# A Mamba-style layer with its chunk outputs laid out by channels instead of by tokens

## The chip, the cores and the metric

The kernel runs on one core of a Trainium2 chip. A core has TensorE (matrix multiply, PE in the profile; its weight loads are shown apart as PEld), VectorE (DVE), ScalarE (ACT), GpSimd (POOL) and SyncE (SP), which here issues the DMAs. The engines run at the same time and wait for each other through semaphores. The metric is the device time of one execution in microseconds (us); lower is better.

## The reference

The input is a batch of 8 images of 64 x 64 pixels with 192 channels. Two layers follow each other. Only the first is concerned; per image its 4096 pixels are a sequence of tokens:

```python
h = layernorm(xs, ln1_w, ln1_b)                  # xs = x + depthwise 3x3 conv
zxbcdt = h @ in_proj_w.T
z, xBC = zxbcdt[..., :384], zxbcdt[..., 384:896]
dt = softplus(zxbcdt[..., 896:] + dt_bias)       # 6 heads
xBC = silu(causal_conv1d(xBC))                   # xm 384, Bm 64, Cm 64
y = ssd(xm, dt, A, Bm, Cm)                       # state-space scan, 6 heads of 64
y = (y + xm * D_skip) * silu(z)
y = y * rsqrt(mean(y * y, -1) + 1e-5) * rms_w
x2 = xs + y @ out_proj_w.T
# then a second 3x3 conv, a layernorm and an MLP (192 -> 768 -> 192, gelu)
```

The scan is done in chunks. Inside a chunk a token's output is the sum over earlier tokens of (C·B) times a decay times dt·x; from the chunks before comes C times the carried state (64 x 64 per head), times the decay since the chunk began. After each chunk the state is decayed and the chunk's own contribution is added.

The second layer (a scan along four directions with another kernel structure) is the same in both kernels.

## The kernel before

**Tiling.** `layer0` goes over 64 tiles of 512 tokens (8 images x 8 tiles); each tile has 4 chunks of 128 tokens. All data are float32. `layer1` then takes the 8 images again.

**Layouts.** Activations lie mostly with channels on the partitions: 96 x 2 for the 192 channels, 128 x 3 for the 384. Some are turned, with the chunk's 128 tokens on the partitions: `zs` (silu of z), `xdt`, and the chunk output.

**One tile**, as a set of generators, with the tiles that the profile names:
- `gate` projects h to z and to the 6 dt columns, chunk by chunk with tokens on the output's partitions (`p_z`, 128 x 390, L531); `keep_gate` adds the dt bias (`dr`, L547) and takes the silu (`zs`, L550).
- `steps_in_time` makes dt (Abs, Exp, Ln), the cumulated decays (`p_c`, L588) and their exponentials `dec`; `rows_of` writes the cumulated sums as rows into a DRAM buffer `csd`, and `decays` loads them back spread over 128 partitions (`e`, L640).
- `powers` and `scores` turn `e` into the 128 x 128 matrix of each head (`e<-e,gm`, L682).
- `turn` transposes the conv output (`p_t`, L699) into `xdt` (L705) and `xw` (L710), and B into `bt`.
- `states` reads the carried state for the chunk (`p_i<-st,cm`, L740), multiplies by the decay (`t1`, L742), and forms the new state (`p_n`, L751; `st`, L761, L764).
- `mixer` forms the chunk output in one PSUM bank `py`: three matmuls with a diagonal matrix `dsk` for the skip term (L787), then six, one per head, with the head's matrix as the stationary operand and 64 columns of `xdt` moving (L790). VectorE adds `t1` (L803) and multiplies by `zs` (L806); ScalarE squares with a running sum (`sqj`, L814).
- `output` waits for the whole tile, computes the norm factor `rq`, scales the four chunk outputs on ScalarE (L843), transposes them back (`p_u`, L850), copies them (`yc`, L859), projects (`p_o`, L873), and adds the residual on VectorE into the padded image `xx` (L883).
- `mlp`, `norm2`, `conv2`, `norm1`, `conv1`, `mix`, `convolve`, `inputs` and `statistics` are the rest of the layer.

**Order.** Nothing is ordered by hand. `Flow` is a planner that runs at build time: every step has an engine, a weight in microseconds, and what it must wait for; buffers are counted slots that are taken and given back (`f.pool`). At each turn the step that can start first is emitted, a rank per generator breaks near-ties, and the order within each engine is then fixed in the program (`keep`). So each engine's queue is strictly in the planned order, and a wrong weight shows as a wait on the chip. `LAG`, `STAY`, `RANK` and the ranks are constants of this planner. PSUM has two pools here: "mm" with 5 banks for 512-column results, and "sm" with 3 banks shared by `p_t`, `p_b`, `p_g`, `p_i`, `p_n`, `p_y`, `p_u` and `p_c`. `xdt`, `xw` and `t1` have one buffer each.

Of the kernel before, what the change touches and what calls it, by code (L numbers as in the profile page):

```python
# [17 lines left out]
TT = 512  # L18
# [170 lines left out]
def layer0(tc, consts, x, x1s, mv1, w_in, w_out, w_fc1, w_fc2, rows):  # L189
# [12 lines left out]
    with ExitStack() as ctx:  # L202
# [39 lines left out]
        nc.vector.tensor_scalar_mul(an, an, -1.0)  # L242

        for i in range(3):
            nc.vector.tensor_scalar_mul(wo[:, i], wo[:, i], v128["rms"][:, i : i + 1])
        dsk = wp.tile([128, 3, 128], F32, name="dsk")
        for i in range(3):
            nc.vector.tensor_scalar_mul(dsk[:, i], ident, v128["dsk"][:, i : i + 1])
# [5 lines left out]

        f = Flow(tc)
        f.LAG, f.STAY, f.RANK = 0.684, -0.464, -0.01
        for tag, n in (("mm", 5), ("sm", 3), ("xin", 2), ("xs", 3), ("h", 3), ("cin", 2), ("cv", 2), ("zs", 2),
                       ("dt", 2), ("e", 5), ("yt", 4), ("yc", 1), ("xx", 3), ("x2", 1), ("m", 1), ("sq", 1), ("s2", 1), ("ld", 3), ("csr", 1), ("xdt", 1), ("xw", 1), ("t1", 1)):
            f.pool(tag, n)
# [255 lines left out]
        def gate():  # L515

            for T in range(len(tiles)):
                yield "wait", ("h1", T)
                yield "take", "zs"
# [3 lines left out]
                zs = got["zs", T] = tp.tile([128, NQ, DIN], F32, name="zs", bufs=2)  # L523
                for c in range(NQ):
# [4 lines left out]
                        1.35,  # L529
                        lambda: [  # L530
                            nc.tensor.matmul(  # L531
                                ps[:, : DIN + NH],
                                h[:, ct, c * Q : c * Q + Q],
                                wi[:, ct, 0 : DIN + NH],
                                start=ct == 0,
                                stop=ct == 1,
# [5 lines left out]
                    if c == NQ - 1:  # L542
                        h1_done(T, r)
                    f.fork(keep_gate(T, c, zs, dr, ps, r))

        def keep_gate(T, c, zs, dr, ps, r):
            q = yield step("DVE", 0.15, lambda: [nc.vector.tensor_add(dr[:, c], ps[:, DIN : DIN + NH], dtb)], r)  # L547
            if last := f.part(("dr", T), NQ, q):
                f.at["dr", T] = last
            r = yield step("ACT", 0.49, lambda: [nc.scalar.activation(zs[:, c], ps[:, :DIN], AF.Silu)], r, "silu")  # L550
            f.give("mm", max(q, r))
            if last := f.part(("zs", T), NQ, r):
                f.at["zs", T] = last

        def steps_in_time():

            for T in range(len(tiles)):
# [6 lines left out]
                    0.8,  # L564
                    lambda: [
                        nc.scalar.activation(dt, dr, AF.Abs),
                        nc.scalar.activation(dt, dt, AF.Exp, scale=-1.0),
# [9 lines left out]
                        nc.vector.scalar_tensor_tensor(dt, dr, 0.0, dt, ALU.max, ALU.add),  # L577
# [11 lines left out]
                        for i, m in enumerate((low, up, ones1))  # L589
# [4 lines left out]
                    "DVE", 0.16, lambda: [nc.vector.tensor_copy(cst.rearrange("p a b -> p (a b)"), pc[:, 24:48])], r  # L594
                )
                f.fork(rows_of(T, da))
                dec = got["dec", T] = sp.tile([128, 3, NQ, NH], F32, name="dec")
# [3 lines left out]
                    lambda: [nc.scalar.activation(dec.rearrange("p a b c -> p (a b c)"), pc[:, 0:72], AF.Exp)],  # L601
# [7 lines left out]
        def rows_of(T, da):  # L609
# [11 lines left out]
            csr = sp.tile([NH, TT], F32, name="csr", bufs=1)  # L621
            r = yield step("ACT", 0.6, lambda: [nc.scalar.copy(csr, ps[:NH])], r)
            f.give("mm", r)
            csd = got["csd", T] = dsp.tile([NH, TT], F32, name="csd")
# [7 lines left out]
        def decays():  # L632

            for T in range(len(tiles)):
                yield "wait", ("cs", T)
                for c in range(NQ):
                    yield "take", "e"
                    e = got["e", T, c] = ch.tile([128, NH, Q], F32, name="e", bufs=5)
                    src = got["csd", T][:, c * Q : c * Q + Q].partition_broadcast(128)
# [83 lines left out]

        def states():

            st = None
            for T, (b, t) in enumerate(tiles):
                yield "wait", ("w2", T)
                yield "wait", ("cv", T)
                dec, cm = got["dec", T], got["cm", T]  # L730
# [38 lines left out]
        def mixer():  # L769

            for T, (b, t) in enumerate(tiles):
# [3 lines left out]
                for c in range(NQ):  # L775
# [19 lines left out]
                    if c == 0:  # L795
                        yield "wait", ("zs", T)
# [1097 lines left out]
```

## Time and profile before

| what | value |
|---|---|
| three runs | 23742.58, 23752.58, 23754.5 us (median 23752.58) |
| the profiled execution | 23759.13 us, of which its span is 23757.4 us |
| busy over the span | PE 21089.6, DVE 21274.2, ACT 21040.0, POOL 16067.4 us |
| first layer: first 4868 us | PE 4496.60, DVE 3899.60, ACT 3178.97, POOL 704.51 us |
| second layer: the other 18889 us | PE 16593.03, DVE 17374.60, ACT 17861.01, POOL 15362.92 us |

The last group of matmuls of the first layer's MLP (L976) begins at 4857.54 us and lasts 10.46 us, and the first instruction of the second layer on GpSimd (L1057) stands at 4868.13 us; that is where the table divides. A float32 matmul appears as two records in the profile, each with its own weight load; a transpose appears as one. "PEclk" is the share of TensorE's clock that the throttle granted.

Durations of neighbouring instructions overlap in the timeline, since the next one starts before the last has drained. Where work follows without a wait, the distance from start to start is what an instruction costs its engine.

### The profile page before, as it was taken

The page shows a single profiled execution, that of the slowest core. Times are in us where ns is not written, and L with a number is a line of the kernel's source. Part 1 is how long each engine was busy: PE and PEld are TensorE (multiplying, and loading weights), DVE is VectorE, ACT ScalarE, POOL GpSimd, SP SyncE. Part 2 cuts the span into 40 slices and gives each one's busy share as a digit, 9 for nine tenths or more (in the row PEclk, how much of TensorE's full clock was granted, in tenths as well). Part 3 has the DMA queues.
Part 4 walks back from the last instruction along what each step waited for, and adds up shares of the span by engine and source line. Part 5 has one row for each costly group of instructions (what it writes and reads, how often), then busy time and mean ns, then how long its engine had stood idle before and what let it go on. Part 6 is the DMA issues. An engine that isn't in the chain of part 4 may idle for free.

```text
span 23757.4 us, 313126 instructions
## 1 busy us (share of the span) xinstructions
PE 21089.6 (89%) x100804; PEld 10279.5 (43%) x100804; DVE 21274.2 (90%) x22093; ACT 21040.0 (89%) x37507; POOL 16067.4 (68%) x12871
## 2 busy tenths in 40 slices
PE   7999999978888888888888888888888888888888
PEld 4444444434444444444444444444444444444444
DVE  7888888779998999899989998999899989998998
ACT  5666766669998999899989998999899989998998
POOL 1111111149995999599959985998699769976997
PEclk8999999989999999999999999999999999999999
DMA  2111111133233323333233233323332233233332
GB/s 50 45 44 44 46 44 43 39 99 81 81 79 107 81 82 78 107 81 82 76 112 81 82 77 109 81 81 79 110 82 81 78 107 82 81 85 100 82 83 67
DMA packets 1368290, 1859.75 MB, mean 78 GB/s; under 512 B 268576, under 2 KB 697024, under 8 KB 1357440
## 3 DMA queue, kind: packets, MB, share of 16 engines
q1 hardware_dynamic: 1366656, 1839.73, 28.7%
q8 instruction: 810, 13.27, 0.2%
q14 instruction: 824, 6.75, 0.1%
HBM read 1225.98 MB, written 210.50 MB: 60 GB/s over the span
## 4 chain that ended last, share of the span: by engine, by line
POOL 43%; PE 24%; ACT 15%; DVE 7%; issue 6%; DMA 4%; SPq 1%; POOLq 0%; ACTq 0%; DVEq 0%
POOL hc L1648 40%; ACT pw L1592 6%; ACT ea L1607 6%; POOL cy L1646 3%; PE p_f L956 3%; DMA xc<-xo 2%; DVE xs L1202 2%; PE p_f L976 2%; PE p_x L448 2%; PE y L1663 2%; PE p_o L873 2%; PE p_y L790 1%; PE g L1618 1%; PE p_d L1481 1%; PE p_z L531 1%
## 5 line engine op out<-in xcount | busy, mean ns | idle before, releaser
L1648 POOL TENSOR_TENSOR hc<-hs,cb 128x1024 f32<-128x1024 f32 x6144 | 14592.9, 2375 | 12.0 <-POOL cy L1646 9.9
L1634 DVE TENSOR_TENSOR_SCAN hs<-ea,cy,g 128x512 f32<-128x512 f32 x10752 | 13024.0, 1262 | 608.6 <-PE g L1618 411.1
L1592 ACT ACTIVATE pw<-duT,bt 128x384 f32<-128x384 f32 x16384 | 8874.1, 601 | 20.2 <-DVE duT L1539 20.2
L1607 ACT ACTIVATE ea<-dr,an 128x512 f32<-128x512 f32 x12288 | 8120.5, 709 | 189.2 <-DVE hs L1634 170.8
L1663 PE MATMUL y<-hc,sel 128*64 128x512 f32 x24576 | 6624.0, 617 | 1841.3 <-POOL hc L1648 1819.2
L1618 PEld LDWEIGHTS g<-ident,pw 128*128 128x128 f32 x49152 | 5288.7, 141 | 4336.8 <-issue 2671.4
L1618 PE MATMUL g<-ident,pw 128*128 128x128 f32 x49152 | 6788.4, 279 | 60.1 <-ACT pw L1592 28.6
L1646 POOL COPY cy<-hs 128x2 f32<-128x2 f32 x6144 | 1164.2, 189 | 3373.5 <-DMA out_x<-xl 1733.8
L1663 PEld LDWEIGHTS y<-hc,sel 128*64 128x64 f32 x24576 | 1225.9, 134 | 3254.1 <-POOL hc L1648 3031.3
L1634 DVE TENSOR_TENSOR_SCAN hs<-ea,g 128x512 f32<-128x512 f32 x1536 | 1763.7, 1202 | 159.0 <-PE g L1618 115.6
L365 POOL TENSOR_TENSOR s<-xs 96x512 f32<-96x512 f32 x64 | 121.1, 1892 | 2033.7 <-DVE xs L343 1522.9
L1202 DVE SCALAR_TENSOR_TENSOR xs<-pad,p,xs 128x4096 f32<-128x4096 f32 x192 | 860.9, 4484 | 43.4 <-ACT xs L1192 36.2
L1510 PE MATMUL p_dt<-xdbl,wd 13*128 13x512 f32 x1536 | 857.2, 639 | 41.0 <-DVE de L1523 39.1
L365 POOL TENSOR_TENSOR s<-sq 96x512 f32<-96x512 f32 x128 | 211.6, 1653 | 964.1 <-ACT sq L378 899.8
L1481 PE MATMUL p_d<-xc,wx 128*44 128x512 f32 x1536 | 791.6, 598 | 22.6 <-DMA xc<-xo 22.0
L343 DVE SCALAR_TENSOR_TENSOR x<-xx,p,x 96x512 f32<-96x512 f32 x1024 | 785.2, 815 | 19.4 <-ACT x L332 19.4
L956 PE MATMUL p_f<-h,wf 96*128 96x512 f32 x1536 | 761.9, 632 | 24.4 <-ACT zs L550 14.0
L343 DVE SCALAR_TENSOR_TENSOR xs<-xin,p,xs 96x512 f32<-96x512 f32 x1024 | 749.3, 767 | 4.6 <-ACT xs L332 4.6
L976 PE MATMUL p_f<-m,wf 128*96 128x512 f32 x1536 | 692.9, 601 | 0.0
L1532 PEld LDWEIGHTS p_du<-ident,de 128*128 128x128 f32 x3072 | 323.5, 141 | 610.2 <-DVE de L1523 405.8
L448 PE MATMUL p_x<-h,wi 96*128 96x512 f32 x1024 | 544.5, 664 | 12.3 <-ACT h L405 11.1
L365 POOL TENSOR_TENSOR s<-x 96x512 f32<-96x512 f32 x64 | 96.2, 1502 | 626.3 <-DVE x L343 477.2
(202 smaller groups left out, 19557.2 us busy)
## 6 DMA issues: line engine op xcount, KB each, us to landing
cb<-cd SPq DMA_DIRECT2D x4096, 128.0 KB
dr<-de SPq DMA_DIRECT2D x3072, 128.0 KB
xc<-xo SPq DMA_DIRECT2D x256, 768.0 KB
e<-csd SPq DMA_DIRECT2D x256, 384.0 KB
xl<-x SPq DMA_DIRECT2D x256, 384.0 KB
ut<-xo SPq DMA_DIRECT2D x128, 768.0 KB
ut<-xo SPq DMA_DIRECT2D x256, 384.0 KB
xo<-xs SPq DMA_DIRECT2D x48, 1024.0 KB
```

Source lines behind the costliest of these rows:

```text
L343: nc.vector.scalar_tensor_tensor(im(out[:, ct]), tap(ct, j), w[:, ct, j : j + 1], im(out[:, ct]), ALU.mult, ALU.add)
L956: nc.tensor.matmul(ps, wf1[:, ct, mt * 128 : mt * 128 + 128], h[:, ct], start=ct == 0, stop=ct == 1)
L976: nc.tensor.matmul(ps[:CP], wf2[:, kt, ct * CP : ct * CP + CP], m[:, kt], start=kt == 0, stop=kt == 5)
L1202: nc.vector.scalar_tensor_tensor(xs, tap(j), kw[:, d, j : j + 1], xs, ALU.mult, ALU.add)
L1481: nc.tensor.matmul(st["p_d"][:44], wx[:, d, k], st["xc"][:, d], start=d == 0, stop=d == DT - 1)
L1592: nc.scalar.activation(st["pw", p, j][:, :, i], st["duT"][:, j].rearrange("p (g c) -> p g c", c=64), AF.Copy, scale=st["bt"][:, j, n : n + 1],
L1607: nc.scalar.activation(ea[:, f], state[s]["dr", d][:, f], AF.Exp, scale=an[:, k, p, at : at + 1])
L1618: nc.tensor.transpose(g[:, f, j * 128 : j * 128 + 128], state[s]["pw", p, j][:, 2 * d + f].rearrange("p a b -> p (a b)"), ident,)
L1634: nc.vector.tensor_tensor_scan(rev(h[:, f]), rev(ea[:, f]), rev(g[:, f]), 0.0 if first(s) else state[s - 1]["cy"][:, p, d, f : f + 1], ALU ...
L1646: o(nc.gpsimd.tensor_copy(st["cy"][:, p, d], h[:, :, last]))
L1648: o(nc.gpsimd.tensor_mul(hc, h, bc(st["cb", p], 1, [128, 2, TT])))
L1663: o(nc.tensor.matmul(y[half[f]], sel, hc[:, f], start=p == 0 and k > 0, stop=p == NP1 - 1))
```

## The change

Only `layer0` changes, and in it six things.

1. **Chunk outputs by channels.** In `mixer`, `xdt` (64 columns of a head) becomes the stationary operand and the head's 128 x 128 matrix moves, so that the result has channels on partitions: 64 rows per head, even heads in rows 0 to 63 and odd heads in rows 64 to 127 of the same 128 columns. The transposes and copies in `output` go.
2. **The carried state in the same bank.** Six more matmuls with the state as stationary operand (64 x 64) add the state's part directly; `p_i` and `t1` go. What moves is C times the decay since the chunk began, one 64 x 128 matrix per head: the new generator `carried` loads the exponentials (`csd` has a second row set for them) over 64 partitions and multiplies them with C on GpSimd, in one buffer `ce`. The state has three buffers, as it is read later.
3. **Skip term on VectorE.** The diagonal matmuls go; three VectorE instructions per chunk form skip times conv output plus bank.
4. **z by channels**, in three groups of 512 tokens; the dt columns get their own matmuls (`p_dr`) with h as the stationary operand.
5. **The norm factor behind the projection.** The squares are summed over channels by a matmul with a matrix of 1/384 (`p_q`), in the new generator `squares`; the factor `rms` multiplies the projected result, and GpSimd adds the residual.
6. dt uses Exp and Ln without Abs; `dec` loses one of its three parts; the planner's constants and ranks are new.

```diff
         f = Flow(tc)
-        f.LAG, f.STAY, f.RANK = 0.684, -0.464, -0.01
+        f.LAG, f.STAY, f.RANK = 0.804, -0.31, -0.01
...
+                        nc.tensor.matmul(
+                            pd[:, c * NH : c * NH + NH],
+                            h[:, ct, c * Q : c * Q + Q],
+                            wi[:, ct, DIN : DIN + NH],
+                            start=ct == 0,
+                            stop=ct == 1,
+                        )
+                        for c in range(NQ)
+                        for ct in range(CT)
...
+                for i in range(3):
...
-                                ps[:, : DIN + NH],
-                                h[:, ct, c * Q : c * Q + Q],
-                                wi[:, ct, 0 : DIN + NH],
-                                start=ct == 0,
-                                stop=ct == 1,
+                                ps, wi[:, ct, i * 128 : i * 128 + 128], h[:, ct], start=ct == 0, stop=ct == 1
...
-                        nc.scalar.activation(dt, dr, AF.Abs),
-                        nc.scalar.activation(dt, dt, AF.Exp, scale=-1.0),
+                        nc.scalar.activation(dt, dr, AF.Exp),
                         nc.scalar.activation(dt, dt, AF.Ln, bias=1.0),
...
-                        nc.vector.scalar_tensor_tensor(dt, dr, 0.0, dt, ALU.max, ALU.add),
+                        nc.vector.scalar_tensor_tensor(dt, dt, BIG, dr, ALU.min, ALU.max),
...
-            r = yield step("ACT", 0.6, lambda: [nc.scalar.copy(csr, ps[:NH])], r)
+            r = yield step(
+                "ACT",
+                1.2,
+                lambda: [nc.scalar.copy(csr[:, 0], ps[:NH]), nc.scalar.activation(csr[:, 1], ps[:NH], AF.Exp)],
+                r,
+                "explog",
+            )
...
+        def carried():
+
+            for T, (b, t) in enumerate(tiles):
+                yield "wait", ("cs", T)
+                yield "wait", ("cv", T)
+                cm = got["cm", T]
+                for c in range(NQ):
+                    if t == 0 and c == 0:
+                        continue
+                    yield "take", "ce"
+                    ce = got["ce", T, c] = ch.tile([NS, NH, Q], F32, name="ce", bufs=CE)
+                    src = got["csd", T][:, 1, c * Q : c * Q + Q].partition_broadcast(NS)
+                    r = yield step("SP", 0.1, lambda: [nc.sync.dma_start(out=ce, in_=src)], f.at["cs", T])
+                    f.at["ce", T, c] = yield step(
+                        "POOL",
+                        2.0,
+                        lambda: [nc.gpsimd.tensor_mul(ce, ce, bc(cm[:, c * Q : c * Q + Q], 1, [NS, NH, Q]))],
+                        r + 3,
+                    )
...
-                        q = yield step("PE", 0.7, lambda: [nc.tensor.matmul(pi, cm[:, tk], st, start=True, stop=True)])
-                        q = yield step(
-                            "DVE", 0.55, lambda: [nc.vector.tensor_mul(hv(t1), hv(pi), bc(dec[:, 1, c], 2, heads))]
-                        )
...
-                        for i in range(3):
-                            cs = slice(i * 128, i * 128 + 128)
-                            f.keep(nc.tensor.matmul(py[:, cs], cv[:, i, tk], dsk[:, i], start=i == 0, stop=False))
-                        for hd in range(NH):
-                            cs = slice(hd * HD, hd * HD + HD)
-                            f.keep(nc.tensor.matmul(py[:, cs], e[:, hd], xdt[:, cs], start=False, stop=hd == NH - 1))
-
-                    q = yield step("PE", 2.2, out)
+                        for w, v in ((xdt, e), (st, ce)):
+                            for hd in range(NH) if w is not None else ():
+                                rows = slice(hd % 2 * 64, hd % 2 * 64 + 64)
+                                cs = slice(hd // 2 * 128, hd // 2 * 128 + 128)
+                                f.keep(
+                                    nc.tensor.matmul(
+                                        py[rows, cs],
+                                        w[:, hd * HD : hd * HD + HD],
+                                        v[:, hd],
+                                        start=w is xdt and hd < 2,
+                                        stop=hd >= NH - 2 and (w is st or st is None),
+                                    )
+                                )
+
+                    q = yield step("PE", 1.3 if st is None else 2.4, out)
...
+                            nc.vector.scalar_tensor_tensor(
+                                yc[:, i, tk], cv[:, i, tk], v128["dsk"][:, i : i + 1], yv[:, i], ALU.mult, ALU.add
+                            )
+                            for i in range(3)
...
+                    q = yield step("DVE", 0.6, lambda: [nc.vector.tensor_mul(yc[:, :, tk], yc[:, :, tk], zs[:, :, tk])])
...
+        def squares():
...
+                    r = yield step("ACT", 0.55, lambda: [nc.scalar.activation(sq, yc[:, :, tk], AF.Square)])
...
+                            nc.tensor.matmul(pq[:CP, tk], onesq, sq[:, i], start=i == 0, stop=i == 2) for i in range(3)
...
+                        nc.scalar.activation(rs, pq[:CP], AF.Ln, bias=eps[:CP]),
+                        nc.scalar.activation(rs, rs, AF.Exp, scale=-0.5),
...
-                    q = yield step("ACT", 0.62, lambda: [nc.scalar.activation(yt, yt, AF.Copy, scale=rs[:, c : c + 1])], r)
...
-                            nc.tensor.transpose(pt[:, i * 128 : i * 128 + 128], yt[:, i * 128 : i * 128 + 128], ident)
...
-                        lambda: [nc.scalar.copy(yc[:, :, c * Q : c * Q + Q], pt.rearrange("p (i q) -> p i q", i=3))],
...
-                        lambda: [nc.vector.tensor_add(xx[:, ct, 1 : RT + 1, 1 : WI + 1], im(ps[:CP]), im(xs[:, ct]))],
+                    r = yield step("DVE", 0.7, lambda: [nc.vector.tensor_mul(inner, im(ps[:CP]), im(rs))], p)
...
+                r = yield step(
+                    "POOL", 2.7, lambda: [nc.gpsimd.tensor_add(both, both, xs.rearrange("p t (h w) -> p t h w", w=WI))]
+                )
```

## The prediction

> **What bounds the kernel now.** I read the busy time by windows first, to see how much of the span the change can touch; then TensorE's timeline over one tile, for prices and gaps; then VectorE and GpSimd beside each other; last the order of the instructions in the two built programs.
>
> ```profile
> core 0: us, PE busy (x) PEld busy (x) DVE busy (x) ACT busy (x) POOL busy (x), PEclk, DMA share, GB/s
> 1000.00:4400.00 3400.00, 3212.36 (x11037) 1593.11 (x11037) 2808.96 (x4643) 2298.83 (x4436) 495.59 (x379) 0.93 0.18 45
> 2500.00:2515.00 15.00, 15.00 (x54) 7.21 (x52) 14.96 (x26) 8.75 (x22) 3.42 (x1) 1.00 0.69 170
> 2515.00:2534.00 19.00, 14.76 (x66) 10.39 (x66) 12.10 (x23) 12.71 (x30) 1.19 (x1) 0.70 0.01 1
> 2534.00:2575.00 41.00, 41.00 (x125) 18.52 (x124) 34.06 (x53) 29.74 (x48) 5.11 (x5) 0.97 0.04 10
> ```
>
> The first row is the steady part of the first layer, 46 tiles in 3400 us: 73.9 us a tile, TensorE busy 69.8 (94%), VectorE 61.1, ScalarE 50.0, GpSimd 10.8. TensorE bounds the layer. The other rows are one tile in three stretches: TensorE is full at full clock in two, and in the middle one it idles for 4.2 of 19 us at 0.70 of the clock. The layer takes 4868 us of 23757; the second layer's instructions don't change, so I price it at nothing.
>
> ```profile
> 2499.70 0.94 PE L787 MATMUL p_y<-dsk,cv 128*128 128x128 f32 x6
> 2500.47 1.45 PE L790 MATMUL p_y<-xdt,e 128*128 128x64 f32 x12
> 2501.85 0.86 PE L751 MATMUL p_n<-xw,bt 128*64 128x384 f32 x2
> 2502.64 0.55 PE L699 MATMUL p_t<-ident,cv 128*128 128x128 f32 x3
> 2503.02 1.02 PE L366 MATMUL ln_m<-s,ones 96*96 96x512 f32 x2
> ...
> 2505.69 0.91 PE L740 MATMUL p_i<-st,cm 64*128 64x384 f32 x2
> 2506.44 0.22 PE L715 MATMUL p_b<-ident,bm 64*128 64x64 f32 x1
> ...
> 2556.20 3.65 PE L448 MATMUL p_x<-h,wi 96*128 96x512 f32 x8
> 2559.69 5.40 PE L531 MATMUL p_z<-wi,h 96*128 96x390 f32 x16
> 2564.93 10.46 PE L976 MATMUL p_f<-m,wf 128*96 128x512 f32 x24
> ```
>
> From start to start, at full clock: the diagonal matmuls 0.77 us a chunk (0.128 a record), the heads 1.38 (0.115 a record, though only 64 columns move), `p_i` 0.75, a transpose 0.38/3 = 0.127, `p_z` 5.24 a tile, a 512-column record 3.49/8 = 0.436.
>
> ```profile
> 2519.83 0.27 PE L715 MATMUL p_b<-ident,bm 64*128 64x64 f32 x1 [0.78 <-DVE xw L710]
> 2522.49 0.69 PE L699 MATMUL p_t<-ident,cv 128*128 128x128 f32 x3 [1.10 <-DVE yt L803]
> 2524.87 1.54 PE L751 MATMUL p_n<-xw,bt 128*64 128x384 f32 x2 [1.06 <-DVE t L742]
> 2528.75 2.66 PE L790 MATMUL p_y<-xdt,e 128*128 128x64 f32 x12
> ```
>
> These rows lie in the middle stretch: `p_t` waits for the bank that `yt` frees, `p_n` for `t1`, and the heads' twelve records take 2.45 us (to 2531.20) instead of 1.38, since the clock has fallen after the gaps. Of such loss a tile has on average 4.1 us of idling and, at 0.93 of the clock, some 0.07 x 69.8 = 4.9 us of slow running.
>
> **What the skill says.** The Trainium skill, "TensorE: Matmul & The Clock Gate", "Part 3: Packing small matmuls", says that the output's start partition picks the column tile and that matmuls in different ones run concurrently. The second layer's `y` shows it: two matmuls of 64 rows each (four records of 512) take 6007.88 - 6006.98 = 0.90 us, as two records of `p_d` alone do (0.96):
>
> ```profile
> 6006.98 1.08 PE L1663 MATMUL y<-hc,sel 128*64 128x512 f32 x4
> 6007.88 1.02 PE L1481 MATMUL p_d<-xc,wx 128*44 128x512 f32 x2
> 6008.84 1.09 PE L1618 MATMUL g<-ident,pw 128*128 128x128 f32 x8
> ```
>
> Its "LDWEIGHTS" section says that a load's time goes with its columns, not its rows; the heads' records above (0.115 us for 64 moving columns behind 128-wide loads, against 0.128 for 128) agree. "SBUF — State Buffer", "Who interferes with whom", says that a VectorE instruction with two SBUF inputs and a GpSimd instruction that reads SBUF exclude each other for their whole length. The trace agrees: a conv step of 0.73 us takes 2.87 when it starts beside a GpSimd add.
>
> ```profile
> 2547.39 2.87 DVE L343 SCALAR_TENSOR_TENSOR xs<-xin,p,xs 96x512 f32<-96x512 f32 x1
> ```
>
> (GpSimd's `xr` add runs from 2547.37 for 2.34 us.) "TensorEngine Tiling (Array Packing)", "Key Properties", says that changing the tiling mode drains the array; `p_n` (64 wide) between 128-wide work takes 0.79 us for 768 columns, 0.65 by the 512-column price, so I put the drain under 0.14 and leave it out.
>
> **The change part by part, per tile.**
>
> TensorE removed: diagonals 4 x 0.77 = 3.1; heads 4 x 1.38 = 5.5; `p_i` 4 x 0.75 = 3.0; transposes `p_u` 12 x 0.127 = 1.5; `p_z` 5.2. Sum 18.3. Added: z by channels 12 records x 0.436 = 5.2; `p_dr` 16 records, each behind a 128-wide load, x 0.115 = 1.8; `p_q` 24 x 0.128 = 3.1; chunk outputs 24 records of 128 columns a chunk. The trace has no 128-column records side by side. If two run together as in `y`: 12 x 0.128 = 1.54 us a chunk, 6.2 a tile; if not, 3.07 and 12.3. I take the first: the column tiles alternate as in `y`, and the loads are half as wide. Added 16.3, or 22.4. Net -2.0 at full clock; divided by 0.93, **-2.2** (else +4.1/0.93 = +4.4).
>
> The loss in the middle stretch, 9.0 us: `p_u`, the ScalarE scaling and copy (twice four of 0.62 and 0.47), `t1` and the wait for the whole tile's norm go, and two users leave the three "sm" banks. Against that, `p_q` holds one of five "mm" banks from the first chunk to the factor. The bound is 0 to -9.0. The chain xdt, heads, bank, next xdt with its one buffer stays, so I take about a third, **-3.3**.
>
> VectorE: `t1` and the add (8 x 0.46, start to start) = -3.7; twelve skip steps of 128 columns at 0.2 (`gm`, the nearest row, starts 0.19 before its successor) = +2.4; three dt adds less, -0.3; the multiplication by `rms` replaces the add at equal size. Net -1.6. But GpSimd gets four `ce` multiplications (64 x 768; between 1.26 us at 512 and 2.34 at 1024 columns: 1.8) and the residual (2.3), 9.5 us with SBUF inputs. Today's 7.4 us of such work cost VectorE, by means over clean durations (16 steps of 0.82 against 0.73, 16 of 0.77, 4 each of `st`, `yt` and `e` 0.1 above theirs, two of `h` 0.08 above), 3.4 us a tile, 0.46 per us. So +4.4, and VectorE ends at 61.1 - 1.6 + 4.4 = 63.9. That is still below TensorE, so most hides; bound 0 to 4.4, I take **+1.0**.
>
> The `ce` loop: the next load may start only when the heads' matmuls have read `ce`; SP waits there with `xin`, `xl` and later loads queued behind it. The cost is the load, 1.8 us on GpSimd (plus a lock) and 1.5 for the matmuls. The nearest load, the first of four `e` twice as large, is issued at 2501.99 and waited for until 2508.26: at most 6.3. So a turn lasts up to 9.6 us. In the changed order the TensorE work between consecutive chunk outputs is, by these prices, about 5.5, 14, 10 and 32 us: only the first gap can be too short, by 0 to 4.1. I take **+0.6**; a load alone and half as large is quicker.
>
> ScalarE loses about 3 us of 50; table loads stay (431 and 427 in the two programs). It was never the bound: nothing beyond the relief above. Fill and drain of the pipeline: nothing.
>
> Sum: -2.2 - 3.3 + 1.0 + 0.6 = -3.9 us a tile, x 64 = -250 us. Against the profiled execution, 23759 - 250 = 23509; the median lies 6.5 lower: **23503**.
>
> **The rivals.**
> - *Heads not side by side* (slower). TensorE then gets +4.4 instead of -2.2: -3.9 + 6.6 = +2.7 a tile, +173: 23926. It decides from 1.54 + 3.9 x 0.93/4 = 2.45 us a chunk on. For it: each head has its own weights to load, where `y` loads the same ones; the planner's own weight for the step, 2.4, fits no overlap. Against: `y`.
> - *Given back on the port*: VectorE's 4.4 and the `ce` stall of 4.1 come in half (4.2 in place of 1.6), and the relief is 2.0: -2.2 - 2.0 + 4.2 = 0: 23753, no change. For it: the conv steps blocked above; against: VectorE has 12.8 us free a tile.
> - *The stretch closes*: 7 of the 9.0 us return, and the charges are 1.2: -8.0 a tile, -512: 23241. For it: the other two stretches run full at full clock; against: `xdt` keeps one buffer.
>
> **How the numbers follow.** Forecast 0.54 (own range 23370 to 23650), heads 0.22, port 0.12, stretch closes 0.12. This measurement can tell about 0.2%, 48 us. Faster: 0.54 + 0.12 + a third of the port case = 0.70; same 0.06; slower 0.22 + the port's other edge = 0.24. The range reaches down to 23260, by the closing stretch, and up to 23880, within the bad cases, leaving some 0.06 below and 0.13 above.
>
> **What would show it.** Right: six pairs of a chunk in some 1.5 us; TensorE busy near 67 us a tile of 70; the clock above 0.93; conv steps (L343) longer on average. Wrong: 24 records spread over 2.5 us or more; TensorE waiting on GpSimd's `ce` in front of the chunk output; tile time unchanged with more idling of TensorE behind VectorE.

## The result and the profile after

The changed kernel takes 24302.43 us (median of four runs, 24289.1 to 24322.3) beside 23753.33 (23742.58 to 23754.5): a ratio of 1.0231, 95% interval 1.0219 to 1.0243. It is 549 us slower where 250 us less were forecast, and the time lies above the range. The view of busy time by windows, divided where the second layer begins, and its steady part:

```profile
core 0: us, PE busy (x) PEld busy (x) DVE busy (x) ACT busy (x) POOL busy (x), PEclk, DMA share, GB/s
0.00:5402.00 5402.00, 4593.28 (x17752) 2242.08 (x17752) 4149.35 (x6537) 2992.88 (x5298) 1429.17 (x862) 0.87 0.21 49
5402.00:24298.90 18896.90, 16602.04 (x85532) 8045.86 (x85532) 17376.19 (x15634) 17871.04 (x31374) 15364.99 (x12323) 0.99 0.31 87
...
1000.00:4400.00 3400.00, 2936.58 (x11365) 1433.15 (x11364) 2695.84 (x4190) 1908.94 (x3395) 918.16 (x539) 0.87 0.21 49
...
2505.00:2518.00 13.00, 13.00 (x52) 5.84 (x50) 3.64 (x6) 6.10 (x10) 2.65 (x3) 1.00 0.11 30
2518.00:2536.00 18.00, 10.46 (x55) 7.00 (x56) 18.00 (x29) 4.45 (x8) 7.27 (x4) 0.57 0.09 23
2536.00:2550.00 14.00, 14.00 (x46) 6.88 (x47) 7.72 (x10) 7.42 (x13) 2.04 (x1) 0.69 0.00 0
```

The first layer has grown from 4868 to 5402 us, the second is the same within 8. In the steady part 41 tiles pass instead of 46: 82.9 us a tile instead of 73.9. TensorE's work has not grown: it is busy for 71.6 us a tile instead of 69.8, but at 0.87 of the clock instead of 0.93; times the clock, as an estimate, that is 62.3 us at full clock instead of 64.9. What has grown is its idling, (3400 - 2936.58)/41 = 11.3 us a tile instead of 4.1, and its slow running, 71.6 - 62.3 = 9.3 instead of 4.9. GpSimd has doubled, 22.4 instead of 10.8. The last three rows show part of one tile: TensorE is full at full clock, then idles for 7.5 of 18 us with a mean clock of 0.57, and is full again with the clock at 0.69.

The timeline from the end of the first of these stretches on (start, duration, line, tiles; in brackets idle time before and what ended it):

```profile
2516.32 0.88 PE L833 MATMUL p_y<-e,xdt 128*64 128x128 f32 x12
2517.12 0.87 PE L833 MATMUL p_y<-ce,st 64*64 64x128 f32 x12
2517.93 1.10 PE L366 MATMUL ln_m<-s,ones 96*96 96x512 f32 x2
...
2519.16 2.25 PE L528 MATMUL p_dr<-wi,h 96*128 96x6 f32 x16
...
2522.49 3.58 POOL L765 TENSOR_TENSOR ce<-ce,cm 64x768 f32<-64x768 f32 x1 [9.52 <-DMA ce<-csd]
...
2526.12 1.54 PE L833 MATMUL p_y<-ce,st 64*64 64x128 f32 x12 [0.94 <-POOL ce L765]
2527.60 1.59 PE L888 MATMUL p_q<-sqc,onesq 128*96 128x128 f32 x6
...
2532.12 7.13 DVE L343 SCALAR_TENSOR_TENSOR xs<-xin,p,xs 96x512 f32<-96x512 f32 x3
2532.31 2.21 POOL L765 TENSOR_TENSOR ce<-ce,cm 64x768 f32<-64x768 f32 x1 [6.24 <-DMA ce<-csd]
2534.48 1.26 POOL L365 TENSOR_TENSOR s<-sq 96x512 f32<-96x512 f32 x1
2535.70 2.34 POOL L975 TENSOR_TENSOR xr<-xr,x 96x1024 f32<-96x1024 f32 x1
2535.79 2.02 PE L366 MATMUL ln_v<-s,ones 96*96 96x512 f32 x2 [6.60 <-POOL s L365]
```

The first three rows answer the question of the heads: both sets of twelve records take 2517.93 - 2516.32 = 1.61 us. Two heads do run side by side. The other rows show what costs. TensorE waits 0.94 us for `ce`, and then 6.60 us for `s`, the sum of squares of a layernorm. `s` has nothing to do with `ce`; it stands behind the next multiplication in GpSimd's queue, and that one waits for its load. The clock is another matter. Windows cut at its steps give 1.00 up to 2520.65 us, 0.50 up to 2544.55 and 1.00 after that. So it fell during the sixteen `p_dr` records, before either wait: TensorE had no gap from 2495.81 to 2525.19 us. It stayed low for 8.8 us after TensorE was full again. The chain of waits gives the same stretch in order (start, duration):

```profile
2516.39 1.63 PE p_y L833 x24
...
2518.07 4.28 DMA ce<-csd
...
2522.49 3.59 POOL ce L765
...
2526.12 1.57 PE p_y L833 x12
...
2527.74 4.41 DMA ce<-csd
...
2534.48 1.27 POOL s L365
...
2535.79 2.02 PE ln_v L366 x2
```

One turn through the single buffer is the load, the multiplication and the matmuls, 2527.74 - 2518.07 = 9.7 us. The waits of the steady part, summed (us in total, times, longest), in the changed kernel:

```profile
POOL ce L765 <- DMA ce<-csd: 1289.5, 138, 21.5
...
PE ln_v L366 <- POOL s L365: 101.5, 25, 7.9
PE p_q L888 <- ACT sqc L883: 65.1, 23, 5.3
PE ln_m L366 <- POOL s L365: 62.0, 16, 8.6
PE p_y L833 <- DVE st L800: 61.2, 18, 5.7
PE p_y L833 <- POOL ce L765: 34.2, 18, 5.2
...
SPq L761 <- PE p_y L833: 1697.8, 135, 45.9
```

and in the kernel before:

```profile
PE ln_v L366 <- POOL s L365: 7.3, 2, 6.8
PE ln_m L366 <- POOL s L365: 6.7, 6, 3.5
```

TensorE waits 34.2 us for `ce` (0.8 a tile) but 101.5 + 62.0 = 163.5 for `s` (4.0 a tile; 14.0 us in the kernel before), and 65.1 for `sqc`, the squares of a chunk output (1.6 a tile). SP stands half of the time before a `ce` load.

### The profile page after: what moved, and what is told of

It is laid out like the page before. It is cut to its first block, busy times and chain, and to the rows that moved or that the text cites. A ratio compares the mean times of both kernels' runs of the same rounds, so it can differ in the third digit from the quotient of the medians.

```text
span 24298.9 us, 318148 instructions
## 1 busy us (share of the span) xinstructions
PE 21195.3 (87%) x103284; PEld 10287.9 (42%) x103284; DVE 21525.5 (89%) x22170; ACT 20863.9 (86%) x36671; POOL 16794.2 (69%) x13184
## 4 chain that ended last, share of the span: by engine, by line
POOL 42%; PE 20%; ACT 17%; DVE 7%; issue 6%; DMA 6%; SPq 2%; POOLq 0%; ACTq 0%; DVEq 0%
POOL hc L1701 37%; ACT pw L1645 7%; ACT ea L1660 7%; POOL cy L1699 3%; DMA xc<-xo 2%; DVE xs L1255 2%; PE p_f L1027 2%; PE y L1716 2%; DMA ce<-csd 2%; PE p_f L1007 2%; PE p_x L448 2%; PE g L1671 1%; PE p_z L558 1%; PE p_y L833 1%; PE p_o L921 1%
## 5 line engine op out<-in xcount | busy, mean ns | idle before, releaser
L1660 ACT ACTIVATE ea<-dr,an 128x512 f32<-128x512 f32 x12288 | 8185.5, 719 | 181.8 <-DVE hs L1687 165.9
L765 POOL TENSOR_TENSOR ce<-ce,cm 64x768 f32<-64x768 f32 x248 | 649.1, 2617 | 2386.0 <-DMA ce<-csd 2047.5
L343 DVE SCALAR_TENSOR_TENSOR xs<-xin,p,xs 96x512 f32<-96x512 f32 x1024 | 856.1, 868 | 85.6 <-ACT xs L332 85.6
L343 DVE SCALAR_TENSOR_TENSOR x<-xx,p,x 96x512 f32<-96x512 f32 x1024 | 845.1, 863 | 38.1 <-ACT x L332 38.1
L1007 PE MATMUL p_f<-h,wf 96*128 96x512 f32 x1536 | 815.6, 668 | 46.6 <-ACT rms L898 18.7
L678 ACT ACTIVATE e<-e,cst 128x128 f32<-128x128 f32 x1536 | 474.8, 389 | 209.2 <-DMA e<-csd 209.1
L497 DVE SCALAR_TENSOR_TENSOR cv<-cin,p,cv 128x512 f32<-128x512 f32 x576 | 482.6, 857 | 120.9 <-ACT cv L482 119.7
```

The lines of the kernel that those rows point to most:

```text
L343: nc.vector.scalar_tensor_tensor(im(out[:, ct]), tap(ct, j), w[:, ct, j : j + 1], im(out[:, ct]), ALU.mult, ALU.add)
L1007: nc.tensor.matmul(ps, wf1[:, ct, mt * 128 : mt * 128 + 128], h[:, ct], start=ct == 0, stop=ct == 1)
L1660: nc.scalar.activation(ea[:, f], state[s]["dr", d][:, f], AF.Exp, scale=an[:, k, p, at : at + 1])
```

## The experiments

All keep the planned order of the changed kernel except where the text says so. The ratio is to the kernel before, run on the same chip, with its 95% interval; the last column is the ratio less one, times 23753. The letters of the theories are those of the expectations, each explained where it comes first.

| run | differs from the changed kernel | median us | ratio | us against before |
|---|---|---|---|---|
| (changed) | | 24302.43 | 1.0231 (1.0219 to 1.0243) | +549 |
| e1 | two `ce` buffers | 24023.44 | 1.0110 (1.0095 to 1.0125) | +261 |
| e2 | no multiplication | 23824.61 | 1.0026 (1.0015 to 1.0036) | +62 |
| e3 | no load | 24020.69 | 1.0113 (1.0096 to 1.0130) | +268 |
| e4 | e1, planner told: new order | 24182.56 | 1.0178 (1.0163 to 1.0194) | +423 |
| e5 | two `ce`, no new GpSimd work | 23716.73 | 0.9988 (0.9982 to 0.9995) | -29 |
| e6 | two `ce`, multiplication on VectorE | 23953.57 | 1.0088 (1.0073 to 1.0103) | +209 |
| e7 | e6, planner told: new order | 24767.11 | 1.0432 (1.0417 to 1.0448) | +1026 |
| e8 | e5 without the load | 23730.51 | 0.9990 (0.9984 to 0.9997) | -24 |
| e9 | e6, loads issued by ScalarE | 24192.06 | 1.0186 (1.0169 to 1.0203) | +442 |
| e10 | kernel before, two other planner constants | 23929.07 | 1.0073 (1.0058 to 1.0088) | +173 |
| e11 | e8, two `xdt` | 23570.09 | 0.9923 (0.9908 to 0.9937) | -183 |
| e12 | e8, no skip term | 23685.40 | 0.9968 (0.9957 to 0.9980) | -76 |
| e13 | two `xdt` | 24205.99 | 1.0187 (1.0172 to 1.0203) | +444 |
| e14 | pairs on VectorE, two `xdt` | 24401.17 | 1.0268 (1.0251 to 1.0285) | +637 |
| e15 | pairs on GpSimd, two `xdt` | 24000.80 | 1.0101 (1.0086 to 1.0116) | +240 |
| e16 | e14, multiplication late in the queue | 23820.15 | 1.0027 (1.0016 to 1.0039) | +64 |
| e17 | e15, multiplication late in the queue | 23835.11 | 1.0033 (1.0021 to 1.0046) | +78 |
| e18 | e16, a second buffer for pairs | 23775.51 | 1.0012 (1.0006 to 1.0019) | +29 |

### The turn and the multiplication: e1, e2, e3

e1 gives `ce` a second buffer that the planner does not know of. To make room, `csr` holds its two row sets on partitions 0 to 5 and 32 to 37, and goes out in two DMAs.

```diff
-ce = ch.tile([NS, NH, Q], F32, name="ce", bufs=CE)
+ce = ch.tile([NS, NH, Q], F32, name="ce", bufs=2)
```

> The order on every engine is that of the changed kernel; only ce has two buffers (the rows csr are laid out smaller to make room, and go out in two DMAs). Theory A, the loop through the one ce buffer (load 4.3 us, GpSimd 2.7, TensorE 1.6, with the layernorm sums queued behind it on GpSimd): most of the 549 us comes back, 23850 to 24000. Theory B, GpSimd's new work locking VectorE's second read port: nothing of that work changes, so 24200 to 24320. Theory C, the plan as a whole (norm factor, squares, the bank that p_q holds): 24200 to 24320 too.

e2 leaves the multiplication out and keeps load and buffer:

```diff
-lambda: [nc.gpsimd.tensor_mul(ce, ce, bc(cm[:, c * Q : c * Q + Q], 1, [NS, NH, Q]))],
+lambda: [],
```

> The multiplication of ce by C on GpSimd is left out (the state's part uses the decays alone), the load stays, everything else in the same order. A: a turn of the loop is 2.7 us shorter and nothing on GpSimd waits for the load any more, so most comes back: 23850 to 24000. B: 7.2 of 9.5 us of new GpSimd work go, so some 3 to 4 us of VectorE's blocking per tile, but where that is hidden as I had taken it, only some 100 us come back: about 24200. C: 24250 to 24320.

e3 leaves the load out; GpSimd multiplies a tile of ones with C instead.

```diff
-lambda: [nc.sync.dma_start(out=ce, in_=src)]
+lambda: []
-nc.gpsimd.tensor_mul(ce, ce, bc(cm[...], 1, [NS, NH, Q]))
+nc.gpsimd.tensor_mul(ce, bc(cone, 1, [NS, NH, Q]), bc(cm[...], 1, [NS, NH, Q]))
```

> The load of ce is left out: GpSimd multiplies C by a constant tile of ones into ce (the decay since the chunk began is left out), same order, same GpSimd work, same port. A: the 4.3 us of the load go from each turn: 23850 to 24000. B: 24250 to 24320, as the GpSimd work stays. C: 24250 to 24320.

A second buffer and no load at all give the same, 288 and 281 us less. Both times lie some 20 us above theory A's range, and little more than half of the 549 us came back instead of most. So it is the turn through one buffer, not the bytes, and it is worth 4.5 us a tile. In e1 TensorE's wait for `ce` is gone and that for `sqc` is 4.7 us instead of 65.1, but that for `s` is still 124.2 (107.7 in e3, where no multiplication waits for a load). Of the waits that went with the turn, the larger part thus lay at the chunk output and its squares, the smaller at `s`.

Without the multiplication 487 us go, and e2 lies below all its ranges. Beyond the turn the multiplication costs at least some 200 us (e1 to e2; e2 still has one buffer). VectorE shows part of why. The sum of what its instructions take above the shortest tenth of their own group (worked out from every record of the steady part) is 3.8 us a tile before, 9.1 in the changed kernel, 9.1 in e1, 11.1 in e3, and 4.8 in e2. It doesn't set the time alone: e3 has 2 us a tile more of it than e1, and the same time.

### Does the order fit? e4, e7, e10

e4 is e1 with the planner told (two buffers, load 5, multiplication 2.7 us); e7 is the same for e6 (below); e10 is the kernel before with two constants of the changed one.

```diff
-f.LAG, f.STAY, f.RANK = 0.684, -0.464, -0.01
+f.LAG, f.STAY, f.RANK = 0.804, -0.31, -0.01
```

> Two ce buffers that the planner knows of, and its weights for the load (5 in place of 3 after issue) and for the multiplication (2.7 in place of 2.0) set to what the trace shows; the order changes. A: TensorE's saving and the shorter chain then come through as forecast: 23450 to 23700. B: above 24000, as the GpSimd work stays. C: 24000 to 24300.

> As e6, but the planner knows of both buffers and of VectorE's work (0.9 us each, load 4.5 us), so that the order is new. Theory A with a plan that fits: below e6, 23650 to 23850 us. Theory C (the constants of the plan fit only the order for which they were chosen; e4 has shown a worse order from better numbers): above e6.

> The kernel before with its work unchanged, and the two planner constants LAG and STAY of the changed kernel (0.804 and -0.31 for 0.684 and -0.464): it measures how much the order of the same instructions is worth. Theory E (each order fits only its own constants, a few hundred us lie in it): 23900 us or more. Theory D (the order matters little, the work and its transfers decide): within 60 us of 23741.

Better numbers for the planner made a worse order each time: 162 us over e1, 817 over e6. And the same instructions in another order cost the kernel before 173 us. An order can be worth more than the whole change that was forecast (250 us), so only runs in one and the same order tell causes apart; all others here keep it. What the best order for the changed kernel would reach is open: only these two others were tried.

### Everything new on GpSimd away: e5, e8

e5 is e1 without the multiplication and without the residual addition (`lambda: []` in both places). e8 also leaves the load out and moves a constant tile of ones.

> Planned order of the changed kernel, two buffers for `ce` (as in e1), and all new GpSimd work left out: the multiplication of the decays with C, and the residual addition of the first layer (so `xx` stays without `xs`; both parts of the computation are missing). Theory A+B (the loop through `ce` costs some 280 us, the new GpSimd work with its lock of the port and its place in GpSimd's queue costs the rest): 23500 to 23650 us, and VectorE's excess over its clean durations returns to about 4 us a tile. Theory C (something else in the plan or in the VectorE work costs it): 23750 us or more, although no GpSimd work is new.

> As e5 (no multiplication with C, no residual addition), and the load of `ce` left out as well: the state's matmuls move one constant tile of ones that nothing waits for. Only TensorE's, VectorE's and ScalarE's new work is left, in the planned order of the changed kernel. Theory D (e5 still paid for the loads, in SP's queue and in the transfers): 23500 to 23600 us, TensorE idle under 4 us a tile. Theory E (the rest of the plan costs it: layernorm sums and the chunk outputs' steps stand late in the queues of VectorE and GpSimd, whatever `ce` does): within 60 us of e5's 23717, with the waits on GpSimd's `s` still there.

e5 missed both of its expectations, and e8 is within 60 us of e5 as theory E said. With nothing left of `ce` but TensorE's matmuls, the changed kernel only equals the one before, though TensorE does less. Its windows (a row of the steady part, then one tile) and its longest waits of TensorE and of VectorE:

```profile
1000.00:4400.00 3400.00, 3160.80 (x12855) 1529.81 (x12853) 2795.55 (x4712) 2159.13 (x3813) 492.17 (x382) 0.91 0.18 44
...
2500.00:2536.00 36.00, 36.00 (x130) 15.90 (x128) 29.70 (x49) 27.24 (x51) 3.41 (x2) 1.00 0.39 91
2536.00:2561.50 25.50, 21.97 (x135) 12.94 (x134) 24.36 (x39) 13.05 (x21) 6.33 (x6) 0.93 0.00 1
2561.50:2572.50 11.00, 10.97 (x22) 4.37 (x23) 7.71 (x16) 6.91 (x11) 0.00 (x0) 0.69 0.00 0
```

```profile
PE ln_v L368 <- POOL s L367: 61.3, 13, 8.0
PE p_f L1009 <- DVE h L401: 37.0, 21, 4.4
PE p_y L835 <- DVE st L802: 27.7, 15, 1.9
...
DVE xdt L732 <- PE p_y L835: 181.0, 106, 7.0
```

TensorE still idles for (3400 - 3160.80)/46 = 5.2 us a tile, at 0.91 of the clock: no relief against 4.1 and 0.93 before. The stretch behind the chunk outputs is still there, with VectorE busy for 24.36 of its 25.5 us, waiting at other times for the one `xdt`. And TensorE still waits 88.5 us for `s` (1.9 a tile), with nothing new on GpSimd: that part of the changed kernel's 4.0 is not the multiplication's.

The clock's steps show something more. In e8's steady part it fell to a half 82 times, and 27 of these times TensorE had had no gap above 0.05 us for 6.8 us. Each of the 27 lies 1.2 to 3.5 us after the start of the new `p_dr` matmuls, sixteen records that move 6 columns each. In the changed kernel it is 8 of 91, with the same neighbour each time; in the kernel before, where `p_z` moves these columns together with 384 others, it is none of 44. An estimate from the busy time at half clock behind the 27 falls is 82 us of 3400, or 1.8 us a tile. No run takes `p_dr` out, so that it pulls the clock down is what the traces suggest, not shown by an experiment.

### What holds the stretch: e11, e12, e13

e11 is e8 with `xdt` in two buffers (`bufs=1` to `bufs=2`), e12 is e8 without the skip term (one VectorE step a chunk instead of four), e13 the complete changed kernel with two `xdt`.

> As e8 (no multiplication, no residual addition, no load of `ce`), with two buffers for `xdt` and the same planned order. In e8 VectorE waits 181 us for `xdt<-p_y` in 3400 (3.9 us a tile). Theory F (the stretch stays open because `xdt` has one buffer, which is the reason that the prediction gave): 23600 us or less, the wait gone. Theory G (VectorE itself is full in that stretch, 24.4 of 25.5 us, with its own work): within 50 us of e8's 23731; the wait on `xdt` shrinks and others of VectorE's queue take its place.

> As e8, with the skip term left out as well: of a chunk's four VectorE steps (three times skip times conv output plus bank, then times silu(z)) one remains, bank times silu(z). That takes some 0.78 us a chunk off VectorE, 3.1 a tile. Theory G (VectorE full in the stretch behind the chunk outputs): at least 2 us a tile less, 23600 us or below. Theory F (the `xdt` buffer): within 60 us of e8's 23731.

> The changed kernel, complete, with two buffers for `xdt` and nothing else changed. In e8 without `ce` the second buffer was worth 160 us. Theory F (the causes add up): 24100 to 24180 us. Theory H (the turn through `ce` holds the chunk outputs anyway, so a free `xdt` only starts the next wait): within 60 us of 24302.

The second `xdt` is worth 159 us (e8 to e11), the missing skip steps 52: theory F holds, and VectorE's own work is a smaller part. In e11 the steady part reads

```profile
1000.00:4400.00 3400.00, 3180.15 (x13227) 1539.41 (x13225) 2889.98 (x4860) 2227.19 (x3942) 543.83 (x396) 0.93 0.19 45
```

with 0.93 of the clock and the wait for `xdt` gone. In the complete kernel the same edit gave 105 us, between the two expectations.

### Complete kernels: e6, e9, e14 to e18

e6 gives the multiplication to VectorE, at the place of GpSimd's; e9 has ScalarE issue the loads.

```diff
-lambda: [nc.gpsimd.tensor_mul(ce, ce, ...)]
+lambda: [nc.vector.tensor_mul(ce, ce, ...)]
```

> Two buffers for `ce`, and the multiplication with C done by VectorE at the place that the plan gives to GpSimd's; nothing left out. VectorE gets four more instructions of about 1 us per tile (+4 us), GpSimd loses 4 x 1.8 and the lock with it. Theory A (loop and lock of GpSimd decide): 23800 to 23950 us, since e2 has shown 23825 with one buffer and no multiplication. Theory C (VectorE's queue is the tight one now, TensorE waits behind it): 24050 us or more.

```diff
-lambda: [nc.sync.dma_start(out=ce, in_=src)]
+lambda: [nc.scalar.dma_start(out=ce, in_=src)]
```

> As e6 (two buffers, multiplication on VectorE, nothing left out), but the loads of `ce` are issued by ScalarE at the place where the plan has SP's, so that they pass the `e` loads, the image loads and the stores that stand in SP's queue, and so that these pass them. Theory D (SP's queue is what couples them): 100 us or more below e6's 23954, the chain's share of the `ce` load falls from 5.7% to under 3%. Theory E: within 60 us of e6. A loss is possible if ScalarE holds on the chunk output of two chunks before: then ScalarE's waits name `p_y`.

e6 is only 52 us under e1 and just over its range. e9 missed: the load's share of the chain of waits rose from 5.7% to 13.4%, and VectorE waited 279.3 us for it in 129 places (70.6 in 26 in e6). None of ScalarE's longest waits names `p_y`; that its loads come late behind its other work is my reading, not shown by a run.

e14 to e18 halve the multiplications: one tile of 128 partitions holds two chunks, and the state alternates between the halves. Load and multiplication are issued with the even chunk. The lines shown are a part of the edit: `csr` is laid out as in e1, and `cp` holds C in two halves, for which ScalarE gets two more instructions a tile.

```diff
+both = ch.tile([128, NH, Q], F32, name="ce", bufs=1)
+half = slice(c % 2 * 64, c % 2 * 64 + 64)
+ce = both[half]
...
+nc.vector.tensor_mul(both[lo:], both[lo:], bc(cp[lo:, c // 2], 1, [128 - lo, NH, Q]))
...
-new = sp.tile([NS, DIN], F32, name="st", bufs=3)
+new = sp.tile([128, DIN], F32, name="st", bufs=3)[slice(0, 64) if c % 2 else slice(64, 128)]
```

> Complete kernel, same planned order: one `ce` tile over 128 partitions holds two chunks (rows 0 to 63 the even, 64 to 127 the odd one, the state alternating between the halves), so that a tile has two multiplications of full width instead of four of half width; they are done by VectorE; `xdt` has two buffers. Two turns a tile through `ce` instead of four, each before a gap of about 14 and 32 us. If turn, GpSimd's multiplication and `xdt` are the whole loss: 2 x 0.95 us more on VectorE than in e11 and the residual on GpSimd back, 23600 to 23720, below the kernel before. If something else in the complete kernel costs: 23800 or more.

> As e14, but the two multiplications of a tile stay on GpSimd (3.6 us a tile instead of 7.2). If the lock and the place in GpSimd's queue are what the multiplication costs (some 200 us for four, e1 to e2), two cost about 100: 23700 to 23820, slower than e14 by some 50 to 100. If VectorE's time is the tighter, e15 is the faster of the two.

e15 lies 309 us under the changed kernel (105 of them by `xdt`, from e13), but e14 is slower than it, with less to multiply. e14's time means, by its expectation, that something else in the complete kernel costs; e15 lies above its range. The VectorE waits of e14 say why, and the timeline of e15 shows GpSimd's other trouble, a multiplication that takes 6.77 us while VectorE goes through a run of steps:

```profile
DVE ce L776 <- DMA ce<-csd: 406.9, 63, 11.0
DVE st L812 <- PE p_n L797: 116.0, 55, 5.1
```

```profile
2543.11 1.40 DVE L343 SCALAR_TENSOR_TENSOR xs<-xin,p,xs 96x512 f32<-96x512 f32 x2
2543.85 6.77 POOL L776 TENSOR_TENSOR ce<-ce,cp 128x768 f32<-128x768 f32 x1 [5.09 <-DMA ce<-csd]
...
2544.44 0.55 DVE L875 TENSOR_TENSOR yc<-yc,zs 128x384 f32<-128x384 f32 x1
...
2544.91 4.05 DVE L343 SCALAR_TENSOR_TENSOR xs<-xin,p,xs 96x512 f32<-96x512 f32 x6
```

In e14 the load holds VectorE's whole queue: 407 of 3400 us. e16 and e17 test it by moving the multiplication, and nothing else: in its engine's queue it now stands directly before the chunk output that reads it.

```diff
 def out():
+    if ("mul", T, c) in got:
+        f.keep(got.pop(("mul", T, c))())
     for w, v in ((xdt, e), (st, ce)):
```

> As e14, complete, but the pair's multiplication stands on VectorE directly before the chunk output that reads it, so that nothing is held behind a load that is still under way. If the wait in the queue is what e14 lost: VectorE's 407 us of waiting for the load fall under 100, and the time to 23700 to 23850. If VectorE's own 2 x 0.95 us or TensorE's new wait for a late multiplication count as much: 24000 or more.

> As e15, complete, with the pair's multiplication on GpSimd directly before the chunk output. If GpSimd's sums `s` behind a multiplication that waits for its load are what e15 still loses: TensorE's waits for `s` (166 us in e15) fall under 100 and the time to 23750 to 23900. If the multiplication's length beside VectorE's two-input steps (up to 6.8 us for 1.8) is what counts: TensorE waits for `ce` instead, 24000 or more.

Two instructions a tile, moved: 573 us less on VectorE, 162 on GpSimd. Both times lie in the ranges expected for a wait in the queue, and so do the waits: in e17 TensorE waits 84.7 us for `s` instead of 165.9, in e16 VectorE waits 0.4 us for the load instead of 406.9. TensorE waits little for the product; in e16:

```profile
PE ln_v L366 <- POOL s L365: 72.9, 15, 8.9
PE p_y L849 <- DVE st L814: 31.9, 15, 2.3
PE p_y L849 <- DVE ce L780: 24.7, 19, 3.0
```

e18 gives the pair a second buffer; B and C of odd chunks lie on rows 64 to 127 for their other uses too, which makes the room.

```diff
-both = ch.tile([128, NH, Q], F32, name="ce", bufs=1)
+both = ch.tile([128, NH, Q], F32, name="ce", bufs=2)
-bm = tp.tile([NS, TT], F32, name="bm", bufs=2)
-cm = tp.tile([NS, TT], F32, name="cm", bufs=2)
+bp = tp.tile([128, 2, Q], F32, name="bp", bufs=2)
```

> As e16, complete (pairs, late multiplication on VectorE, two `xdt` buffers, same planned order), with two buffers of a pair each; the room comes from keeping B and C of even chunks on rows 0 to 63 and of odd chunks on rows 64 to 127 instead of twice on rows 0 to 63. If SP standing before `ce` loads still costs: ScalarE's waits for the `e` loads (138 us in e16, 42 in e8) fall below 70, and the time to 23640 to 23740, below the kernel before. If what is left is VectorE's own added time: within 40 us of e16's 23820.

SP's longest waits in it no longer name the loads of `ce` (L773) behind a chunk output:

```profile
SPq L657 <- ACT csr L651: 1082.0, 88, 47.2
SPq L1068 <- DVE xr L1055: 887.1, 45, 48.8
SPq L303 <- DVE xs L343: 660.8, 55, 44.7
SPq L672 <- PE p_y L850: 39.0, 6, 8.3
SPq L773 <- DMA csd<-csr: 27.9, 21, 2.6
```

That was worth about 35 us more, and ScalarE's waits for `e` fell only from 138 to 94; both halves of its expectation were missed, it lies between them. So SP's queue, which the prediction had named, is a small part in these kernels. e18 is the best complete version of the change: of its 549 us, 520 are gone, at a ratio of 1.0012. No complete version tried here beat the kernel before.

## Why the prediction was wrong, step by step

The forecast was -3.9 us a tile and the result is 549/64 = +8.6, 12.5 more. The two charges for `ce` and for GpSimd's work, +0.6 and +1.0, measured +9.0 together: 7.4 too little, and enough alone to make the change slower. The relief of the stretch accounts for the other 5.1.

- **TensorE, -2.2 us a tile: held.** At full clock, by the estimate above, 62.3 us a tile instead of 64.9, -2.6 against -2.0 in the sum; a chunk takes 1.61 us instead of 1.54. The first rival fell. The Trainium skill, "TensorE: Matmul & The Clock Gate", "Part 3: Packing small matmuls", holds for heads with weights of their own, which `y` could not show.
- **The `ce` loop, +0.6: this is the step that failed.** The length of a turn came out (9.6 worked out, 9.7 measured), by luck: the load took 4.3 us instead of 6.3, the multiplication 3.6 instead of 1.8. TensorE's direct wait was about right, 0.8 us a tile. But the working asked only when the chunk output would be late, and named SP's queue as the one behind the wait. It did not go on through the other queues. A late chunk output makes its squares late, and TensorE waits for those too (1.6 us a tile, 0.1 in e1). On GpSimd the multiplication waits for the load with layernorm's sums `s` behind it, and TensorE waits for those: 4.0 us a tile in all, of which 1.9 stay without any new work there (e8) and 2.8 with two buffers (e1). The turn is worth 4.5 us a tile (e1, e3) in place of 0.6, and everything new on GpSimd together with the turn (549 + 24)/64 = 9.0 (e8). That a multiplication waiting in a queue costs what stands behind it is shown in the kernels with pairs: moved in its queue, it is worth 162 us on GpSimd (e15 to e17) and 573 on VectorE (e14 to e16).
- **VectorE and the port, +1.0: too small a share was charged.** The lock itself was sized well: +4.4 us a tile was worked out, and VectorE's excess rose by 5.3, from 3.8 to 9.1. "So most hides" was the error: free time on average says nothing about the stretch in which VectorE's result is awaited, and the timeline above has it held for 7.13 us over three steps there. The multiplication costs at least some 200 us beyond the turn (e1 to e2), 3.1 a tile; how that divides between lock and queue wasn't separated. With two buffers it and the residual addition cost 290 together (e1 to e5).
- **The relief of the stretch, -3.3: it did not come.** e8 has no `ce` charge at all and should have shown -2.2 - 3.3 = -5.5 a tile; it shows -24/64 = -0.4, so this term was +1.8. The reason that the prediction itself set against a fuller relief, the one `xdt`, is 2.5 of it (e8 to e11, 159/64). With it gone, -183/64 = -2.9 a tile are reached. The working also priced `p_dr` by its records alone, 1.8 us a tile, and its effect on the clock at nothing; the falls of the clock behind it in e8 are worth an estimated 1.8 more, not shown by a run and not simply to be added to the 2.5. What keeps the rest is open: the order was planned with other costs, and e10 shows how much an order can hold, but no run isolates it.
- **The sum** is -2.2 + 1.8 + 9.0 = +8.6 a tile, times 64 = 550 us. It closes by the way the terms were taken: e8 divides the whole loss in two, and the -2.2 is the forecast's own.
- **The signs to look for** did show it: TensorE waiting for `ce`, a lower clock, and conv steps longer (L343 for `xs` 868 ns on average instead of 765). The clock was the plainest, 0.87 where more than 0.93 had been forecast.
- **The rivals.** "Given back on the port" was nearest in kind, but its `ce` stall was priced at the turn's direct wait too. The case that came, a wait that holds others in its queue, was not among them.

## What to carry to other kernels

When an instruction gets a new wait, list what stands behind it in its engine's own queue and who waits for that; the reader of its result may be the least of it. Put such an instruction as late in the queue as its reader allows (573 and 162 us here), and try a second buffer for what it writes (288). Free time on average hides nothing in a stretch where the next matmul waits for exactly that engine. Look at the steps of TensorE's clock beside its gaps: here most falls had idling just before them (83 of 91 in the changed kernel), but some came while TensorE was full, right behind matmuls that move few columns.

## What the runs showed of the hardware

- The exclusion of VectorE and GpSimd works both ways. The Trainium skill, "SBUF — State Buffer", "Who interferes with whom", calls the shared ports an exclusive lock. The traces agree, and here the wait outlasted several instructions: three GpSimd instructions in a row kept a VectorE step waiting for all three (three `xs` steps in 7.13 us, the middle one of them 5.81, 0.73 each when alone), and a run of VectorE steps in e15 kept a GpSimd multiplication of 1.8 us for 6.77. The longest `ce` multiplication in the changed kernel took 7.78 us.
- The row of 24 records in 1.61 us is for weights that differ from head to head: 0.067 us a record of 128 columns when two column tiles alternate, beside 0.128 for full-width records.
- A 192 KB load from a few rows of DRAM, spread over 64 partitions, took 4.3 us alone. In e6 one took 12.0 us; three `e` loads of 384 KB each had been issued in the same queue in the 1.7 us before it.
- TensorE's granted clock moved between 1.00 and 0.50. In the kernel before it was at a half from 2522.75 to 2536.40 us, with no gap above 1.10 us since 2515. In the changed kernel it fell at 2520.65 us after 25 us without a gap, behind sixteen records of 6 columns, and came back 8.8 us after the last gap had ended.
